# TensorE products with few contract rows are given 128 rows, the added ones zero

## The chip, the cores and the metric

The kernel runs on one core of a Trainium2 chip. The metric is the device time of one execution in microseconds (us). The times compared are those of executions without a profile; a profiled execution of this kernel is longer, and its page and trace serve to see what happens inside.

## What is computed

There are 16 graphs (B) of 1,024 nodes (N) with 64 features each (C). Cut to what matters, for each graph:

```python
h = maximum(layernorm(x), 0)
neigh = (adj > 0) & ~eye                      # neighbours of each node
rank = cumsum(neigh, -1) - neigh              # number of a neighbour along its row
nb = neigh.sum(-1)
skip = where(nb > 10, (nb + 1) // 2, 1)       # at least 1
rem = neigh & (skip > 1) & (rank % skip == skip - 1) & mask
rem = rem | transpose(rem)                    # edges dropped, in both directions
nd = (adj or eye) and not rem
s = sort(where(nd, h, inf))                   # per node and feature, over the neighbours left
agg = 0.25 * quantile(s, 0.25) + 0.5 * quantile(s, 0.5) + 0.25 * quantile(s, 0.75)
y = relu((h + agg) @ W1 + b1) @ W2 + b2       # 64 -> 128 -> 64
out = x + y * mask
```

The kernel does not sort dense rows. It turns each node's remaining neighbours into a short list of indices, gathers their features from a table in memory, and sorts those.

## The kernel before

The kernel is one program in which two streams are woven together: the preparation of the next graphs (load, number, drop, keep, order, collect) and the results of the graphs before (sorting networks on VectorE, then the dense layers). A scheduler fixes the order on each engine when the program is built. P is 128, NT is 8 (row tiles of a graph), HALF is 512, KEYS is 136 and PACKED is 332 columns.

The cuts below are the parts that the change and the prediction touch. A comment "L702" gives the line number under which the profile names the statement; these comments are added here.

Constants. `base` is zero outside its first two rows, and zero in those from column 136 on; `blocks` is 1 where the row's number is less than the column's; `ones16` is all ones, and in the program each has 128 rows.

```python
b2r = cst.tile([1, C], F32, name="b2r")
ones_r = cst.tile([1, P], F32, name="ones_r")
...
ident16, ones16, minus16, before16, base, blocks, own2 = (...)
```

Loading a graph: the sign of the adjacency, transposed by TensorE, with the diagonal taken off.

```python
nc.scalar.activation(sg, at, AF.Sign)                                   # L640
...
    nc.tensor.matmul(tp[:, s], sg[:, m * P:(m + 1) * P], ident16, ...)  # L646
if t // 4 == n:
    nc.tensor.matmul(tp[:, t % 4], minus16, ident16, ...)               # L651
...
nc.scalar.activation(to, tp, AF.Relu, saturate=False)                   # L656, to ne
```

Counting the neighbours of each node in each block of 128 columns (`cnt`, 8 rows) and in all (`nb`):

```python
counts[b] = wk.tile([NT, N], BF16, name="cnt", bufs=1)
...
for s in range(NT):
    nc.tensor.matmul(cp, one[:, 7 - s:15 - s], ne[:, s, cols], ...)     # L674
nc.scalar.copy(cnt[:, cols], cp)                                        # L675
...
for t in range(lo, hi):
    nc.tensor.matmul(nb[:, t:t + 1], cnt[:, t * P:(t + 1) * P], ones16[0:NT, 0:1], start=True, stop=True)  # L678
```

Dropping edges: a neighbour's number in its row is the count of the blocks before it (8 rows) and its number within the block.

```python
for n in range(2):
    rk = psum.tile([P, HALF], F32, name="rk", tag="mx", bufs=3)
    nc.tensor.matmul(
        rk, cnt[:, ts], blocks[0:NT, 4 * n:4 * n + 4, None].to_broadcast([NT, 4, P]), start=True, stop=False, ...
    )                                                                   # L702
    for s in range(4):
        nc.tensor.matmul(rk[:, s * P:(s + 1) * P], ne[:, 4 * n + s, ts], upper, ...)   # L707
    nc.scalar.activation(dist[:, n * HALF:(n + 1) * HALF], rk, AF.Abs, bias=...)       # L711
nc.vector.tensor_scalar(rem[:, t], dist, 1.0, half[:, t:t + 1], OP.add, OP.is_equal)   # L712
```

Collecting: the packed codes of each node's neighbours are put into the order of their numbers, on top of a base of keys (2 rows). VectorE takes the indices out of it.

```python
flat = psum.tile([P, PACKED], F32, name="codeP", tag="code", bufs=2)
nc.tensor.matmul(flat, ones16[0:2], base[0:2], start=True, stop=False)  # L790
for t in range(NT):
    nc.tensor.matmul(flat, perm[:, t, k * P:(k + 1) * P], pack[:, t], start=False, stop=(t == NT - 1))  # L792
nc.scalar.copy(st[:, k], flat[:, OWN:VALUES])                           # L795, then L799 and L800
...
nc.vector.max(keys[:, at:at + 8], left)                                 # L805
```

Gathers and sorting: `nc.gpsimd.indirect_dma_start` (L930) gathers one list place of 128 nodes; VectorE sorts (L961, L962), weighs (L969) and TensorE sums (L971).

The dense layers:

```python
for t in range(NT):
    nc.tensor.matmul(high, o[:, t, 0:2 * C], at[:, t], ...)             # L1051
for t in range(NT):
    nc.tensor.matmul(low, o[:, t, 2 * C:], at[:, t], ...)               # L1054, 64 columns
highs = wk.tile([P, HALF], F32, name="highs", bufs=1)
nc.scalar.copy(highs, high)
lows = wk.tile([C, HALF], F32, name="lows", bufs=1)
nc.scalar.copy(lows, low)
hp = psum.tile([P, HALF], F32, name="hp", tag="misc")
nc.tensor.matmul(hp, w1, highs, start=True, stop=False)                 # L1061
nc.tensor.matmul(hp, w1[0:C], lows, start=False, stop=True)             # L1062, 64 rows
...
nc.tensor.matmul(yp, ones_r, b2r[:, None, :].to_broadcast([1, n, C]), start=True, ...)  # L1074, 1 row
for k in range(n):
    nc.tensor.matmul(yp[:, k], h1[:, k * P:(k + 1) * P], w2, ...)       # L1078
```

A float32 matmul stands in the trace as two records, so the 32 products at L1061 are 64 there.

Of the kernel before, what the change touches and what calls it, by code (L numbers as in the profile page):

```python
# [27 lines left out]
F32 = mybir.dt.float32  # L28
F16 = mybir.dt.float16
BF16 = mybir.dt.bfloat16  # L30
# [9 lines left out]
P = 128  # L40
N = 1024
C = 64
H = 128
NT = N // P
# [490 lines left out]
def list_layer(  # L535
# [65 lines left out]
    w1 = cst.tile([P, H], F32, name="w1")  # L601
    w2 = cst.tile([H, C], F32, name="w2")
    b1c = cst.tile([H, 1], F32, name="b1c")
    b2r = cst.tile([1, C], F32, name="b2r")
    ones_r = cst.tile([1, P], F32, name="ones_r")

    def late_constants():

        nc.sync.dma_start(out=kf, in_=cf32[:, F32_AT:F32_AT + F32_PARTS[-1]])
        for n in range(2):  # L610
            nc.sync.dma_start(out=w1[n * C:(n + 1) * C], in_=W1)
        nc.sync.dma_start(out=w2, in_=W2)
        nc.sync.dma_start(out=b1c, in_=b1[:, None])
        nc.sync.dma_start(out=b2r, in_=b2[None, :])
        nc.vector.memset(ones_r, 1.0)

    over = cst.tile([P, 3, B, NT], F32, name="over")
# [5 lines left out]
    neT, nbs, rems, perms = {}, {}, {}, {}  # L623
    pack = cst.tile([P, NT, PACKED], BF16, name="pack")
    nc.vector.tensor_copy(pack[:, :, OWN:OWN + 2], own2.rearrange("p (t k) -> p t k", k=2))
    lists, owns, coefs, tables = {}, {}, {}, {}
    group_idx, group_own, group_num, group_tab, counts = {}, {}, {}, {}, {}

    def load(b, fast=False):

        ne = wk.tile([P, NT, N], FP8, name="ne", bufs=2)
        neT[b] = ne

        counts[b] = wk.tile([NT, N], BF16, name="cnt", bufs=1)
        nbs[b] = [wk.tile([P, NT], F32, name=n) for n in ("bias", "half")]
        for t in range(NT):
            ask(b, t)
            at = asked.pop((b, t))
            sg = wk.tile([P, N], BF16, name="sg")
            nc.scalar.activation(sg, at, AF.Sign)  # L640
            ask(*divmod(b * NT + t + 2, NT))
            for n in range(2):
                tp = psum.tile([P, 4, P], F32, name="tp", tag="mx", bufs=3)
                for s in range(4):
                    m = 4 * n + s
                    nc.tensor.matmul(  # L646
                        tp[:, s], sg[:, m * P:(m + 1) * P], ident16, start=(s == 0), stop=(s == 3 and t // 4 != n),
                        skip_group_check=True,
                    )
                if t // 4 == n:  # L650
                    nc.tensor.matmul(tp[:, t % 4], minus16, ident16, start=False, stop=True, skip_group_check=True)  # L651
                to = ne[:, 4 * n:4 * n + 4, t * P:(t + 1) * P]
                if fast:
                    nc.vector.tensor_scalar(to, tp, 0.0, None, OP.max, saturate=False)
                else:
                    nc.scalar.activation(to, tp, AF.Relu, saturate=False)  # L656
            if fast and t == 3:
                number(b, 0, 4)
            yield 0.1
        if fast:  # L660
            number(b, 4, NT)
        else:
            number(b, 0, NT)
        yield 1.4

    def number(b, lo, hi):

        ne, cnt = neT[b], counts[b]
        bias, half = (k[:, lo:hi] for k in nbs[b])
        for n in range(lo // 4, hi // 4):  # L670
            cols = slice(n * HALF, (n + 1) * HALF)
            cp = psum.tile([NT, HALF], F32, name="cp", tag="mx", bufs=3)
            for s in range(NT):
                nc.tensor.matmul(cp, one[:, 7 - s:15 - s], ne[:, s, cols], start=(s == 0), stop=(s == NT - 1))  # L674
            nc.scalar.copy(cnt[:, cols], cp)  # L675
        nb = psum.tile([P, NT], F32, name="nb", tag="misc")
        for t in range(lo, hi):
            nc.tensor.matmul(nb[:, t:t + 1], cnt[:, t * P:(t + 1) * P], ones16[0:NT, 0:1], start=True, stop=True)  # L678
        nb = nb[:, lo:hi]

        sk = wk.tile([P, NT], I32, name="sk")[:, lo:hi]
        nc.vector.tensor_scalar(sk, nb, 1.0, None, OP.add)
        many = wk.tile([P, NT], F32, name="many")[:, lo:hi]
        nc.vector.scalar_tensor_tensor(many, nb, 10.0, mask[:, b, lo:hi], OP.is_gt, OP.mult)
        nc.vector.tensor_scalar(sk, sk, 1, None, OP.logical_shift_right)
        nc.vector.tensor_scalar(bias, sk, -1.5, -2047.0, OP.mult, OP.add)
        nc.vector.tensor_scalar(half, sk, 0.5, 1.0, OP.mult, OP.add)
        nc.vector.tensor_tensor(half, half, many, OP.mult)

    def drop(b):  # L690

        ne = neT[b]
        bias, half = nbs[b]
        cnt = counts[b]
        rem = wk.tile([P, NT, N], BF16, name="rem", tag="wide", bufs=1)
        rems[b] = rem
        for t in range(NT):
            ts = slice(t * P, (t + 1) * P)
            dist = wk.tile([P, N], F16, name="dist")
            for n in range(2):  # L700
                rk = psum.tile([P, HALF], F32, name="rk", tag="mx", bufs=3)
                nc.tensor.matmul(  # L702
                    rk, cnt[:, ts], blocks[0:NT, 4 * n:4 * n + 4, None].to_broadcast([NT, 4, P]), start=True, stop=False,
                    skip_group_check=True,
                )
                for s in range(4):
                    nc.tensor.matmul(  # L707
                        rk[:, s * P:(s + 1) * P], ne[:, 4 * n + s, ts], upper, start=False, stop=(s == 3),
                        skip_group_check=True,
                    )  # L710
                nc.scalar.activation(dist[:, n * HALF:(n + 1) * HALF], rk, AF.Abs, bias=bias[:, t:t + 1])  # L711
            nc.vector.tensor_scalar(rem[:, t], dist, 1.0, half[:, t:t + 1], OP.add, OP.is_equal)  # L712
            yield 0.5
# [59 lines left out]
    def collect(b, parts=((0, NT),)):  # L773
# [12 lines left out]
        for first, last in parts:  # L786
            for k in range(first, last):
                flat = psum.tile([P, PACKED], F32, name="codeP", tag="code", bufs=2)
                code = flat[:, :KEYS].rearrange("p (s k) -> p s k", k=17)
                nc.tensor.matmul(flat, ones16[0:2], base[0:2], start=True, stop=False)  # L790
                for t in range(NT):
                    nc.tensor.matmul(  # L792
                        flat, perm[:, t, k * P:(k + 1) * P], pack[:, t], start=False, stop=(t == NT - 1)
                    )
                nc.scalar.copy(st[:, k], flat[:, OWN:VALUES])  # L795
                halves, bytes_ = (
                    own[:, k, b % 2].bitcast(d).rearrange("p (c k) -> p c k", c=C) for d in (BF16, U8)
                )
                nc.scalar.copy(halves[:, :, 1], flat[:, VALUES:VALUES + C])  # L799
                nc.scalar.copy(bytes_[:, :, 0:2], flat[:, VALUES + C:].rearrange("p (c k) -> p c k", k=2))  # L800
                left = code[:, :, :16]
                rest = wk.tile([P, NT, 16], F32, name="rest", bufs=1)
                lo, hi = PASSED[k], PASSED[k + 1]
                for at in range(lo, hi, 8):
                    nc.vector.max(keys[:, at:at + 8], left)  # L805
                    if at + 8 < hi:
                        nc.vector.match_replace(rest, keys[:, at:at + 8], left, 0.0)
                        left = rest
                yield 0.4 * (hi - lo) / 4 - 0.4
# [231 lines left out]
    def mlp(b, o):  # L1041
# [3 lines left out]
        for n in range(2):  # L1045
# [8 lines left out]
                nc.tensor.matmul(low, o[:, t, 2 * C:], at[:, t], start=(t == 0), stop=(t == NT - 1))  # L1054
            highs = wk.tile([P, HALF], F32, name="highs", bufs=1)
            nc.scalar.copy(highs, high)
            lows = wk.tile([C, HALF], F32, name="lows", bufs=1)
            nc.scalar.copy(lows, low)
            yield 1.0
            hp = psum.tile([P, HALF], F32, name="hp", tag="misc")  # L1060
            nc.tensor.matmul(hp, w1, highs, start=True, stop=False)  # L1061
            nc.tensor.matmul(hp, w1[0:C], lows, start=False, stop=True)  # L1062
            h1 = wk.tile([P, HALF], F32, name="h1", bufs=1)
            nc.scalar.activation(h1, hp, AF.Relu, bias=b1c)
            yield 1.0
# [5 lines left out]
    def output(h1, n, mask, x):  # L1071

        yp = psum.tile([P, n, C], F32, name="yp", tag="misc")
        nc.tensor.matmul(  # L1074
            yp, ones_r, b2r[:, None, :].to_broadcast([1, n, C]), start=True, stop=False, skip_group_check=True
        )
        for k in range(n):
            nc.tensor.matmul(  # L1078
                yp[:, k], h1[:, k * P:(k + 1) * P], w2, start=False, stop=(k == n - 1), skip_group_check=True
            )  # L1080
        nc.vector.tensor_tensor(yp, yp, mask[:, :, None].to_broadcast([P, n, C]), OP.mult)
        nc.vector.tensor_tensor(x, x, yp, OP.add)
# [323 lines left out]
```

## Time and profile before

| what | value |
|---|---|
| device time, median of 3 | 2027.63 us |
| lowest and highest | 2026.68 and 2040.0 us |
| span of the profiled execution | 2713.0 us |
| mean granted TensorE clock in it | 0.688 of full speed |

In the profile, PE is TensorE's matmuls and PEld its weight loads, DVE is VectorE, ACT is ScalarE, POOL is GpSimd and SP the engine that issues most transfers. A group's line reads: source line, engine, operation, output<-inputs, stationary rows*columns, rows x columns of the moving operand, type and count; then the busy time in us and the mean of one in ns; then the idle time of the engine ahead of it, and what ended most of it. In a timeline the first two numbers are the start and the duration in us; a bracket gives the idle time ahead on that engine. In records, the clock of TensorE is either full or half, and changes about every few to some hundred us. The chain is the work that ended last, followed back from the end through what released each step; "issue" in it is time in which an engine waited for nothing that the profile shows.

### The profile page before, as it was taken

What the parts mean: (1) busy time and instruction counts of PE and PEld (TensorE: products, weight loads), DVE (VectorE), ACT (ScalarE), POOL (GpSimd) and SP (SyncE); (2) the same over time, 40 slices, a digit from 0 to 9 for tenths busy, and PEclk for the clock granted to TensorE, in tenths of its full rate; (3) what the DMA queues carried; (4) which work ended last, traced back from release to release, by engine and by line L of the source; (5) the groups of instructions that cost most, each with busy time, mean ns of one, the idle gap of its engine ahead of it and who ended that gap; (6) DMA issues with size and microseconds to landing.
All of it is one profiled execution on the core that took longest, in us unless ns stands there. A gap on an engine that the chain in (4) does not pass through costs nothing.

```text
span 2713.0 us, 25381 instructions
## 1 busy us (share of the span) xinstructions
PE 1377.2 (51%) x8367; PEld 737.9 (27%) x8385; DVE 1162.5 (43%) x3634; ACT 926.9 (34%) x2414; POOL 1128.6 (42%) x1129
## 2 busy tenths in 40 slices
PE   7227163433664655645564555643565665514435
PEld 3114132211332323322232333322332323202223
DVE  2202255232322752453523652466633554338692
ACT  6247243323552533243342544232341532100101
POOL 0630726353325454455525355445325345537100
PEclk7657576665776767766687767756677677656767
DMA  3232212021222231212212121222111211111000
GB/s 99 64 79 72 59 47 61 14 71 45 78 53 47 48 84 24 67 49 66 48 37 59 43 73 37 55 65 49 53 42 24 62 23 19 30 22 22 20 0 11
DMA packets 152591, 130.12 MB, mean 48 GB/s; under 512 B 117570, under 2 KB 118082, under 8 KB 152450
## 3 DMA queue, kind: packets, MB, share of 16 engines
q1 hardware_dynamic: 116482, 91.51, 12.1%
q0 software_dynamic: 35968, 36.90, 8.0%
q8 instruction: 68, 1.11, 0.2%
q14 instruction: 73, 0.60, 0.1%
HBM read 112.78 MB, written 13.81 MB: 47 GB/s over the span
## 4 chain that ended last, share of the span: by engine, by line
PE 37%; another core or an unknown queue 33%; issue 11%; ACT 10%; DVE 8%; DMA 1%; POOL 0%; SPq 0%; POOLq 0%; DVEq 0%; ACTq 0%
PE codeP L792 6%; PE rk L707 3%; PE acc L971 3%; PE rk L702 3%; PE kp L727 2%; PE kp L724 2%; ACT dist L711 2%; PE kp L723 2%; PE tp L646 2%; ACT sg L640 2%; PE low L1054 2%; PE high L1051 2%; PE cp L674 2%; DVE g L962 2%
## 5 line engine op out<-in xcount | busy, mean ns | idle before, releaser
L930 POOL DMA_INDIRECT g<-htab,idx x1072 | 1072.7, 1001 | 1324.7 <-issue 376.7
L646 PE MATMUL tp<-kb,sg 128*128 128x128 bf16 x1024 | 123.4, 270 | 400.6 <-issue 138.4
L961 DVE TENSOR_TENSOR g<-g 128x768 f32<-128x768 f32 (+3 forms) x408 | 279.5, 702 | 88.1 <-DMA g<-htab,idx 81.2
L962 DVE TENSOR_TENSOR g<-g 128x512 f32<-128x512 f32 (+3 forms) x408 | 279.3, 701 | 20.2 <-PE tp L651 10.7
L711 ACT ACTIVATE dist<-rk,bias 128x512 f16<-128x512 f32 x256 | 172.4, 690 | 329.2 <-remote 188.9
L712 DVE TENSOR_SCALAR rem<-dist,half 128x1024 bf16<-128x1024 f16 x128 | 62.8, 491 | 421.6 <-ACT dist L711 387.2
L656 ACT ACTIVATE ne<-tp 128x512 fp8e4<-128x512 f32 x240 | 136.3, 600 | 310.8 <-remote 214.2
L971 PE MATMUL acc<-g,kf 128*128 128x256 f32 (+2 forms) x448 | 155.0, 495 | 162.1 <-DVE g L969 120.4
L702 PE MATMUL rk<-kb,cnt 8*128 8x512 bf16 x256 | 126.0, 492 | 176.6 <-ACT dist L711 100.8
L646 PEld LDWEIGHTS <-sg 128*128 128x128 bf16 x1024 | 93.0, 123 | 428.8 <-issue 244.1
L792 PE MATMUL codeP<-pack,perm 128*128 128x332 bf16 x1024 | 201.3, 342 | 9.5 <-DVE pause L941 6.3
L728 ACT ACTIVATE kept<-kp 128x512 fp8e4<-128x512 f32 x256 | 151.8, 600 | 122.7 <-remote 87.9
L731 PE MATMUL code<-kw,kept 128*128 128x17 fp8e5 x1024 | 67.3, 175 | 172.3 <-ACT kept L728 95.7
L971 PEld LDWEIGHTS acc<-g,kf 128*128 128x128 f32 x448 | 96.3, 256 | 191.5 <-DVE g L969 125.6
L707 PEld LDWEIGHTS <-ne 128*128 128x128 fp8e4 x1024 | 75.1, 114 | 262.2 <-issue 261.3
L640 ACT ACTIVATE sg<-at 128x1024 bf16<-128x1024 f32 x128 | 132.6, 1055 | 13.3 <-DMA at<-in_adj_dram 13.3
L792 PEld LDWEIGHTS <-perm 128*128 128x128 bf16 x1024 | 95.9, 106 | 150.0 <-issue 84.3
L707 PE MATMUL rk<-kw,ne 128*128 128x128 fp8e5 x1024 | 131.6, 265 | 0.0
L805 DVE MAX8 keys<-codeP 128x8 f32<-128x128 f32 x128 | 38.0, 297 | 205.2 <-ACT own L800 128.6
L1032 DVE TENSOR_SCALAR at_p<-iota,node 128x512 bf16<-128x512 f16 x256 | 77.4, 360 | 111.3 <-remote 86.9
L795 ACT CAST st<-codeP 128x4 bf16<-128x4 f32 x128 | 21.4, 167 | 294.6 <-PE codeP L792 139.9
L727 PE MATMUL kp<-kw,rem 128*128 128x128 fp8e5 x1024 | 118.0, 239 | 0.0
(155 smaller groups left out, 2315.2 us busy)
## 6 DMA issues: line engine op xcount, KB each, us to landing
at<-in_adj_dram SPq DMA_DIRECT2D x128, 512.0 KB
g<-htab,idx POOLq DMA_INDIRECT x1072
xt<-in_x_dram SPq DMA_DIRECT2D x16, 256.0 KB
htab<-xt SPq DMA_DIRECT2D x16, 256.0 KB
gtab<-xt SPq DMA_DIRECT2D x16, 256.0 KB
y<-in_x_dram SPq DMA_DIRECT2D x16, 256.0 KB
out_dram<-y SPq DMA_DIRECT2D x16, 256.0 KB
gg<-g SPq DMA_DIRECT2D x16, 96.0 KB
```

The source lines that it names most:

```text
L640: nc.scalar.activation(sg, at, AF.Sign)
L646: nc.tensor.matmul(tp[:, s], sg[:, m * P:(m + 1) * P], ident16, start=(s == 0), stop=(s == 3 and t // 4 != n), skip_group_check=True,)
L702: nc.tensor.matmul(rk, cnt[:, ts], blocks[0:NT, 4 * n:4 * n + 4, None].to_broadcast([NT, 4, P]), start=True, stop=False, skip_group_check= ...
L707: nc.tensor.matmul(rk[:, s * P:(s + 1) * P], ne[:, 4 * n + s, ts], upper, start=False, stop=(s == 3), skip_group_check=True,)
L711: nc.scalar.activation(dist[:, n * HALF:(n + 1) * HALF], rk, AF.Abs, bias=bias[:, t:t + 1])
L727: nc.tensor.matmul(kp[:, s], rem[:, t, at:at + P], minus, start=False, stop=(s == 3))
L728: nc.scalar.activation(kept[:, 4 * n:4 * n + 4], kp, AF.Relu, saturate=False)
L792: nc.tensor.matmul(flat, perm[:, t, k * P:(k + 1) * P], pack[:, t], start=False, stop=(t == NT - 1))
L930: nc.gpsimd.indirect_dma_start(out=g[:, slot, k - lo, h], out_offset=None, in_=tab, in_offset=bass.IndirectOffsetOnAxis(ap=idx[:, at:at + ...
L961: nc.vector.tensor_tensor(at(f, df, n), pa, pb, one)
L962: nc.vector.tensor_tensor(pa if back else pb, pa, pb, other)
L971: nc.tensor.matmul(acc, ident32, lines[:, s], start=False, stop=(s == now[-1] and not ends), skip_group_check=True)
```

## The change

Each product whose stationary operand had 1, 2 or 8 rows, and the one with 64, gets an operand of 128 rows; the rows added hold zeros in one of the two factors, so that the product is the same. For that, `cnt`, `lows` and `b2r` become constants that are cleared once and of which only the first rows are written. The base product of the keys no longer writes the 196 columns in which it is zero, 136 instead of 332. It is for TensorE to see products of one shape. The 64-row products of the small group at the end (L1134) are left as they are, as are those with few stationary columns (L674, L1054).

```diff
-    b2r = cst.tile([1, C], F32, name="b2r")
-    ones_r = cst.tile([1, P], F32, name="ones_r")
+    b2r = cst.tile([P, C], F32, name="b2r")
+    nc.vector.memset(b2r, 0.0)
+    ones_r = cst.tile([P, P], F32, name="ones_r")
+    lows = cst.tile([P, HALF], F32, name="lows")
+    nc.vector.memset(lows, 0.0)
...
-        nc.sync.dma_start(out=b2r, in_=b2[None, :])
+        nc.sync.dma_start(out=b2r[0:1], in_=b2[None, :])
...
+    cnt = cst.tile([P, N], BF16, name="cnt")
+    nc.vector.memset(cnt, 0.0)
...
-        counts[b] = wk.tile([NT, N], BF16, name="cnt", bufs=1)
...
-            nc.scalar.copy(cnt[:, cols], cp)
+            nc.scalar.copy(cnt[0:NT, cols], cp)
...
-            nc.tensor.matmul(nb[:, t:t + 1], cnt[:, t * P:(t + 1) * P], ones16[0:NT, 0:1], start=True, stop=True)
+            nc.tensor.matmul(nb[:, t:t + 1], cnt[:, t * P:(t + 1) * P], ones16[:, 0:1], start=True, stop=True)
...
-                    rk, cnt[:, ts], blocks[0:NT, 4 * n:4 * n + 4, None].to_broadcast([NT, 4, P]), start=True, stop=False,
+                    rk, cnt[:, ts], blocks[:, 4 * n:4 * n + 4, None].to_broadcast([P, 4, P]), start=True, stop=False,
...
-                nc.tensor.matmul(flat, ones16[0:2], base[0:2], start=True, stop=False)
+                nc.tensor.matmul(
+                    flat[:, :KEYS], ones16, base[:, :KEYS], start=True, stop=False, skip_group_check=True
+                )
                 for t in range(NT):
                     nc.tensor.matmul(
-                        flat, perm[:, t, k * P:(k + 1) * P], pack[:, t], start=False, stop=(t == NT - 1)
+                        flat, perm[:, t, k * P:(k + 1) * P], pack[:, t], start=False, stop=(t == NT - 1),
+                        skip_group_check=True,
                     )
...
-            lows = wk.tile([C, HALF], F32, name="lows", bufs=1)
-            nc.scalar.copy(lows, low)
+            nc.scalar.copy(lows[0:C], low)
...
-            nc.tensor.matmul(hp, w1[0:C], lows, start=False, stop=True)
+            nc.tensor.matmul(hp, w1, lows, start=False, stop=True)
...
-            yp, ones_r, b2r[:, None, :].to_broadcast([1, n, C]), start=True, stop=False, skip_group_check=True
+            yp, ones_r, b2r[:, None, :].to_broadcast([P, n, C]), start=True, stop=False, skip_group_check=True
```

More of the change, by code (lines that the diff above doesn't have):

```diff
@@ L625, in list_layer @@
     nc.vector.tensor_copy(pack[:, :, OWN:OWN + 2], own2.rearrange("p (t k) -> p t k", k=2))
+    cnt = cst.tile([P, N], BF16, name="cnt")
+    nc.vector.memset(cnt, 0.0)
     lists, owns, coefs, tables = {}, {}, {}, {}
-    group_idx, group_own, group_num, group_tab, counts = {}, {}, {}, {}, {}
+    group_idx, group_own, group_num, group_tab = {}, {}, {}, {}
     def load(b, fast=False):
@@ L666, in number @@
     def number(b, lo, hi):
-        ne, cnt = neT[b], counts[b]
+        ne = neT[b]
         bias, half = (k[:, lo:hi] for k in nbs[b])
@@ L693, in drop @@
         bias, half = nbs[b]
-        cnt = counts[b]
         rem = wk.tile([P, NT, N], BF16, name="rem", tag="wide", bufs=1)
```

## The prediction

> **What bounds the kernel now.** I first read the page's table of engines: no engine is busy for more than half of the profiled span, so no sum of busy time can be the time.
>
> ```profile
> span 2713.0 us, 25381 instructions
> PE 1377.2 (51%) x8367; PEld 737.9 (27%) x8385; DVE 1162.5 (43%) x3634; ACT 926.9 (34%) x2414; POOL 1128.6 (42%) x1129
> ```
>
> One warning goes with it: the profiled execution took 2713 us, the timed ones 2027.63. Some 686 us of the profile are the recording's own. I therefore take from the profile durations and intervals of single instructions, which repeat to a few ns, and not shares of the span.
>
> Second I read the chain that ended last, to see which engine's work is on the path.
>
> ```profile
> PE 37%; another core or an unknown queue 33%; issue 11%; ACT 10%; DVE 8%; DMA 1%; POOL 0%; SPq 0%; POOLq 0%; DVEq 0%; ACTq 0%
> PE codeP L792 6%; PE rk L707 3%; PE acc L971 3%; PE rk L702 3%; PE kp L727 2%; PE kp L724 2%; ACT dist L711 2%; PE kp L723 2%; PE tp L646 2%; ACT sg L640 2%; PE low L1054 2%; PE high L1051 2%; PE cp L674 2%; DVE g L962 2%
> ```
>
> Among the engines TensorE carries the chain: 37% of 2713 us are 1004 us, nearly three quarters of its 1377 us of busy time. The two dearest places are the ones that the change edits: codeP (L790, L792) and rk (L702, L707). The 44% under an unknown queue or "issue" are time in which the profile names no worker; where the missing 686 us lie I can't tell, but this is the likely place.
>
> Third I read the groups by form, for the narrow products and their neighbours.
>
> ```profile
> L792 PE MATMUL codeP<-pack,perm 128*128 128x332 bf16 x1024 | 201.3, 342 | 9.5 <-DVE pause L941 6.3 <-DVE perm L769 2.6 <-issue 0.4
> L707 PE MATMUL rk<-kw,ne 128*128 128x128 fp8e5 x1024 | 131.6, 265 | 0.0
> L702 PE MATMUL rk<-kb,cnt 8*128 8x512 bf16 x256 | 126.0, 492 | 176.6 <-ACT dist L711 100.8 <-issue 51.1 <-ACT ne L656 24.4
> L790 PE MATMUL codeP<-kb 2*128 2x332 bf16 x128 | 42.2, 330 | 116.8 <-DVE keys L805 40.6 <-issue 39.1 <-DVE rest L807 35.2
> ```
>
> The form "8*128" is 8 stationary rows by 128 columns. A mean of one matmul is the latency of a pipelined instruction, so I price by intervals between starts, from the timeline. First a stretch at half clock, matmuls and then weight loads:
>
> ```profile
> 1005.08 0.61 PE L707 MATMUL rk<-kw,ne 128*128 128x128 fp8e5 x4
> 1005.48 1.06 PE L646 MATMUL tp<-kb,sg 128*128 128x128 bf16 x8
> 1006.33 0.31 PE L651 MATMUL tp<-kb 128*128 128x128 bf16 x1
> 1006.58 0.60 PE L702 MATMUL rk<-kb,cnt 8*128 8x512 bf16 x1
> 1007.11 0.61 PE L707 MATMUL rk<-kw,ne 128*128 128x128 fp8e5 x4
> 1007.65 0.60 PE L702 MATMUL rk<-kb,cnt 8*128 8x512 bf16 x1
> ...
> 1006.23 0.15 PEld L651 LDWEIGHTS <-kb 128*128 128x128 bf16 x1
> 1006.57 0.10 PEld L702 LDWEIGHTS <-cnt 8*128 8x128 bf16 x1 [0.20 <-issue]
> 1007.11 0.34 PEld L707 LDWEIGHTS <-ne 128*128 128x128 fp8e4 x4 [0.44 <-issue]
> ```
>
> Eight 128-row matmuls of 128 columns take 1006.33 - 1005.48 = 0.85 us, 0.106 each; the load of L651 begins 0.10 us ahead of its matmul, so it lies beside the previous one. The single L651 ahead of L702 takes 1006.58 - 1006.33 = 0.25 us: 0.14 too much. The load of L702 begins only with its own matmul (1006.57, after 0.20 us without a load). L702 itself, 512 columns, takes 0.53 us where four times 0.106 are 0.43: 0.10 too much, and again the next load (L707) waits until 1007.11. One narrow matmul costs about 0.24 us more than a full one of the same columns.
>
> Then a stretch at full clock:
>
> ```profile
> 700.97 1.31 PE L792 MATMUL codeP<-pack,perm 128*128 128x332 bf16 x8
> 702.22 0.31 PE L790 MATMUL codeP<-kb 2*128 2x332 bf16 x1
> 702.46 1.31 PE L792 MATMUL codeP<-pack,perm 128*128 128x332 bf16 x8
> 703.70 0.31 PE L790 MATMUL codeP<-kb 2*128 2x332 bf16 x1
> ```
>
> L790 to L792 takes 0.24 us. The median between two adjacent L792 of the same columns, counted over 690 pairs at full clock, is 143 ns; so 0.10 is excess after the narrow matmul, and 702.22 - 700.97 = 1.25 against 8 x 0.143 = 1.14 shows 0.10 before it.
>
> **What the Trainium skill says.** "TensorEngine Tiling (Array Packing)", section "Key Properties": changing the tiling mode, not just the tile, drains TensorE. It gives no duration; that a matmul of few rows changes the mode by itself is my reading, and the excess on both sides in the trace agrees with it. "TensorE: Matmul & The Clock Gate", section "LDWEIGHTS (loading the stationary operand)": a load goes by its columns, and 32 rows load no faster than 128. The trace agrees: 94 ns on average for L702's 8 rows, 106 for L792's 128. The same page, "What happens when you issue a matmul", says that the next weights are loaded during the running matmul, which is what the loads between full matmuls do and those at a narrow one don't. Its "Back-to-back issue gap" has a matmul paid by its moving columns; so more rows of zeros should cost nothing.
>
> **The change, part by part.** Excess per narrow matmul, as medians of intervals in the whole trace (in, out):
> - L702, 8 rows, x256. Half clock: in 246 - 107 = 139 ns, out 535 - 427 = 108; together 247. Full clock: in 152 - 56 = 96, out 317 - 216 = 101; together 197. Of the 232 that L707 follows at once, 132 ran at half clock (57%): mean 225 ns, x256 = 58 us.
> - L790, 2 rows, x128. Full clock: 94 + 99 = 193; half: 140 + 111 = 251; 78% at full clock: 206 ns, 26 us. Its columns fall from 332 to 136: 196 columns at 143/332 = 0.43 ns are 84 ns at full, 275/332 = 0.83 make 162 at half clock; mean 101 ns, 13 us. The t = 0 matmul over all 332 columns is unchanged.
> - L1074, 1 row, 34 pairs: in 309 - 216 = 93, out 304 - 216 = 88; 6 us. L1062, 64 rows, 32 pairs: from L1061 523 ns, where L1061 to itself has 533: no gain inside; out 522 - 427 = 95; 3 us. Float32 loads there are exposed anyway.
> - L678, 8 rows, 16 groups: L674 has 8 columns, L678 needs 128, so a change of form stays between them (312 against 216 ns). One change out is saved at most: 2 us. L1054 with its 64 columns (309 against 216 after L1051) stays as it is.
> - Added: three clears, about a microsecond of VectorE at the start while inputs arrive.
>
> Sum: 58 + 26 + 13 + 6 + 3 + 2 = 108 us of TensorE time. What lies on the path? Of L702 and L707 the chain holds 78 + 84 of 126 + 132 us, 63%; of L790 and L792 27 + 153 of 42 + 201, 74%; about 70% for the rest. So 58 x 0.63 = 36, 39 x 0.74 = 29, 11 x 0.7 = 8: 73 us.
>
> From this I take a fifth, because of the first rival, and predict 58 us: 2027.6 - 58 = 1970 us.
>
> **What moves.** The instructions are the same in number but for the clears; their order is not. Set side by side, about 2,500 of VectorE's 6,475 and 1,700 of ScalarE's 2,843 stand elsewhere, and in TensorE's queue the runs of L1051 go from 70 to 81, of L1054 from 50 to 72, of L971 from 83 to 71. The scheduler gives narrow matmuls another price, and the weaving of two batches comes out differently. Queues run in order, so a worse weave costs waits anywhere. For this I allow 20 to 30 us either way.
>
> **Rivals.**
> First, ScalarE takes over in the drop stage. For one tile there it does two dist (690 ns), two ne (600) and one sg (1055): 3.6 us. TensorE needs 2 x (0.53 + 0.54) + 0.96 = 3.1 us at half clock. If it holds throughout, the 58 us of rk are hidden and some 37 us remain on the path: about 1990. For it: rk waits 100.8 us for dist. Against it: from 1001 to 1009 TensorE is busy for 7.10 of 8 us and ScalarE for 5.61, and ne or sg isn't there for every tile.
> Second, GpSimd's gathers are the bound: 1,072 of them at 1,001 ns. Then at most the last stages gain: about 2010. For it: it works while the others stand still (858 to 869). Against: it also waits long for VectorE's idx (300.7 us), and the chain holds no POOL.
> Third, zeros aren't free or the new weave is bad: 2030 to 2060. Nothing in the profile shows a row's price; I hold the weave possible and small.
> Fourth, the waits that a late TensorE causes in two woven streams multiply: all 108 us and more come back, 1900 to 1920. TensorE's share of the chain supports it mildly.
>
> **Range and chances.** 1970 in the middle; the weave and the first rival give a spread of about 35 us: 1920 to 2016 should hold it 8 times in 10. The mark for 2% is 1987, half a spread away: faster 0.69, within 2% 0.25, slower 0.06.
>
> **What would show it.** In the changed profile the load of L702's successor should begin ahead of its matmul, with no 0.20 and 0.44 us before loads; L702 to L707 should be 216 or 427 ns, L790 to L792 about 60 or 115 ns, and TensorE's busy time should fall by roughly 100 us. Wrong would be the mechanism if those intervals stay; wrong would be the path if they shrink and the time doesn't, and then ScalarE's or GpSimd's row should be unchanged in the waits; the weave is to blame if waits appear at lines without any narrow matmul.

## Result: 2030.68 to 1976.03 us, and the profile after

| kernel | device time, median | ratio to before, 95% interval |
|---|---|---|
| before | 2030.68 us | |
| after | 1976.03 us | 0.9725, 0.9678 to 0.9772 |

The gain is 55 us, or 2.75%.

Two views of the kernel after show what became of the narrow products. First the timeline at half clock, in a stretch like the one that the prediction read (matmuls, then weight loads; start and duration in us, then the instruction; L702 and L707 are now L706 and L711, L646 and L651 are L651 and L656):

```profile
145.62 0.31 PE L656 MATMUL tp<-kb 128*128 128x128 bf16 x1
145.73 0.63 PE L706 MATMUL rk<-kb,cnt 128*128 128x512 bf16 x1
146.15 0.63 PE L711 MATMUL rk<-kw,ne 128*128 128x128 fp8e5 x4
146.58 0.63 PE L706 MATMUL rk<-kb,cnt 128*128 128x512 bf16 x1
...
145.62 0.15 PEld L706 LDWEIGHTS <-cnt 128*128 128x128 bf16 x1
145.73 0.15 PEld L711 LDWEIGHTS <-ne 128*128 128x128 fp8e4 x1
146.15 0.36 PEld L711 LDWEIGHTS <-ne 128*128 128x128 fp8e4 x3 [0.28 <-issue]
```

The load of L706 begins at 145.62, together with the matmul before its own; the first load of L711 begins with L706. From L656 to L706 it is 0.11 us (before: 0.25), from L706 to L711 0.42 (before: 0.53). One group of rk goes from 1.07 to 0.85 us. What matters is which load lies beside which matmul, not whether a bracket stands there: the 0.28 us ahead of the last three loads lies beside L706 itself, and no matmul is late for it. It is so in the whole traces: the load of L702 begins within 20 ns of its own matmul in 168 of 174 pairs that follow a 128-row matmul closely (counted in before_again, below), while that of L706 is never less than 53 ns ahead, in 157 pairs.

Then the timeline at full clock in the collect stage (L790 and L792 are now L794 and L798):

```profile
770.78 1.30 PE L798 MATMUL codeP<-pack,perm 128*128 128x332 bf16 x8
771.92 0.22 PE L794 MATMUL codeP<-kb 128*128 128x136 bf16 x1
771.98 1.30 PE L798 MATMUL codeP<-pack,perm 128*128 128x332 bf16 x8
```

A base product and its eight followers take 1.20 us (771.98 - 770.78) where they took 1.49.

The whole-trace medians say the same. L706 to L711 is 215 ns at full clock and 426 at half (were 317 and 535), L794 to L798 59 at full clock (was 242; 160 in the run below in which only its columns fall, so about 100 of the 183 belong to the rows). L711 to L706 is 107 ns at half clock (was 247). At full clock it is 56 where the two follow at once (was 152); many pairs stand at 106 or about 197 there, though the weights are loaded as early in them, so that what they wait for is something else.

Now the page of after: engines, and the chain.

```profile
span 1979.1 us, 25408 instructions
PE 1147.2 (58%) x8369; PEld 705.8 (36%) x8385; DVE 1167.4 (59%) x3637; ACT 912.2 (46%) x2414; POOL 1165.0 (59%) x1129
POOL 0372753777377776777767776762777377771000
PE 7%; POOL 5%; DVE 5%; issue 4%; DMA 1%; ACT 0%; POOLq 0%; DVEq 0%
```

This span is that of the timed runs, while the profile of before shown ahead of the prediction was 686 us longer than its own, so the two can't be subtracted. The row of POOL's busy tenths differs as well. In that profile it was

```profile
POOL 0630726353325454455525355445325345537100
```

and now it is 7 in most slices, which is all that a closed line of gathers can show, 1.03 us busy in each 1.33. The chain adds up to 22% only and ends early; it is of no use for shares here.

### The profile page after: what moved, and what is told of

It is laid out like the page before. It is cut to its first block, busy times and chain, and to the rows that moved or that the text cites. A ratio compares the mean times of both kernels' runs of the same rounds, so it can differ in the third digit from the quotient of the medians.

```text
span 1979.1 us, 25408 instructions
## 1 busy us (share of the span) xinstructions
PE 1147.2 (58%) x8369; PEld 705.8 (36%) x8385; DVE 1167.4 (59%) x3637; ACT 912.2 (46%) x2414; POOL 1165.0 (59%) x1129
## 5 line engine op out<-in xcount | busy, mean ns | idle before, releaser
L937 POOL DMA_INDIRECT g<-htab,idx x1072 | 1108.3, 1034 | 610.0 <-issue 313.0
L798 PE MATMUL codeP<-pack,perm 128*128 128x332 bf16 x1024 | 175.9, 312 | 33.4 <-DVE pause L948 32.0
L651 PE MATMUL tp<-kb,sg 128*128 128x128 bf16 x1024 | 109.5, 247 | 107.5 <-ACT sg L645 90.6
L728 PE MATMUL kp<-rem,kw 128*128 128x512 bf16 x256 | 99.2, 388 | 99.9 <-DVE rem L716 53.2
L798 PEld LDWEIGHTS <-perm 128*128 128x128 bf16 x1024 | 91.8, 99 | 135.9 <-issue 48.8
L731 PEld LDWEIGHTS <-rem 128*128 128x128 bf16 x1024 | 81.3, 98 | 147.4 <-issue 105.3
L706 PE MATMUL rk<-kb,cnt 128*128 128x512 bf16 x256 | 110.1, 430 | 38.0 <-ACT dist L715 24.4
L651 PEld LDWEIGHTS <-sg 128*128 128x128 bf16 x1024 | 82.7, 112 | 131.2 <-ACT sg L645 100.5
L711 PEld LDWEIGHTS <-ne 128*128 128x128 fp8e4 x1024 | 88.5, 108 | 89.2 <-issue 65.1
L1058 PE MATMUL high<-at_p,o 128*128 128x512 bf16 x240 | 69.6, 401 | 81.6 <-DVE at_p L1039 80.5
L711 PE MATMUL rk<-kw,ne 128*128 128x128 fp8e5 x1024 | 115.0, 239 | 0.0
L990 ACT CAST o<-acc 128x512 bf16<-128x512 f32 x48 | 28.3, 589 | 179.2 <-PE acc L978 171.1
```

The costliest lines, as they stand in the source:

```text
L731: nc.tensor.matmul(kp[:, s], rem[:, t, at:at + P], minus, start=False, stop=(s == 3))
L937: nc.gpsimd.indirect_dma_start(out=g[:, slot, k - lo, h], out_offset=None, in_=tab, in_offset=bass.IndirectOffsetOnAxis(ap=idx[:, at:at + ...
```

## Experiments

Twelve runs, of nine kernels, were made in four sets; in two of these the unchanged kernel took 2031 and 2032 us and in the other two 2673 and 2675 us, so a ratio is compared only with ratios of the same kind of set, and each table below is of one kind.

### The kernel before once more

No edit.

> The kernel before once more, unchanged, for a second profile of it. If the 686 us by which the first profiled span was longer than the timed runs were the recording's own, this span is near 2030 us, the share of an unknown queue in the chain falls from 33% to under 5%, and GpSimd's gathers then stand as closely as after the change, 1.33 us from start to start. The rival, that the gaps belong to the kernel's order, has them again at the same places. Time ratio 1.00 in both.

Measured: 1.0005 (0.9984 to 1.0026), a span of 2026.5 us. Page of this run (engines, POOL's tenths, chain):

```profile
span 2026.5 us, 25381 instructions
PE 1286.0 (63%) x8367; PEld 709.0 (35%) x8385; DVE 1166.2 (58%) x3634; ACT 913.8 (45%) x2414; POOL 1159.4 (57%) x1129
POOL 0371762777165777577747776771757777770000
PE 13%; POOL 8%; issue 5%; DVE 4%; ACT 1%; DMA 1%; POOLq 0%; DVEq 0%
```

The unknown queue is gone from the chain, and GpSimd's gathers stand closely. This is the profile that after is to be compared with. TensorE's busy time falls from 1286.0 to 1147.2, by 139 us; the others hardly move (DVE +1, ACT -2, POOL +6). But the span falls by 47. The groups that issue gathers (L930, L1143) and the VectorE group that sorts what they bring (L961) show what became of it (busy us, mean ns, then the idle time of the engine ahead of them and what ended it). Before:

```profile
L930 POOL DMA_INDIRECT g<-htab,idx x1072 | 1105.6, 1031 | 654.2 <-issue 316.4 <-DVE idx L834 166.4 <-DVE at_p L1032 75.2
L1143 POOL DMA_INDIRECT out_dram<-gx,gto x4 | 4.8, 1204 | 191.4 <-DMA out_dram<-y 185.8 <-PE kp L727 2.8 <-DMA out_dram<-gx,gto 2.5
L961 DVE TENSOR_TENSOR g<-g 128x768 f32<-128x768 f32 (+3 forms) x408 | 280.2, 702 | 374.7 <-DMA g<-htab,idx 367.3
```

After:

```profile
L937 POOL DMA_INDIRECT g<-htab,idx x1072 | 1108.3, 1034 | 610.0 <-issue 313.0 <-DVE idx L841 166.2 <-PE tp L651 67.8
L1149 POOL DMA_INDIRECT out_dram<-gx,gto x4 | 4.1, 1026 | 182.6 <-DMA out_dram<-y 179.3 <-DMA out_dram<-gx,gto 3.0 <-issue 0.3
L968 DVE TENSOR_TENSOR g<-g 128x768 f32<-128x768 f32 (+3 forms) x408 | 280.4, 703 | 430.3 <-DMA g<-htab,idx 423.9
```

The 1,072 gathers cost 1106 and 1108 us, plus some 315 us at 0.30 us of "issue" between two: 1.33 us from start to start, unchanged. GpSimd's idle time in these two groups falls from 845.6 to 792.6 us, by 53, and the span by 47. What got shorter are the waits ahead of a new batch of gathers, for lists and for free buffers (with the engines named by inference, so I read their sum only), and the wait at the end for the last outputs (186 to 179 us). The first gather begins at 74.6 us instead of 80.8. So the time is a line of gathers with fixed pitch, its waits for the rest, and a tail. This sum alone doesn't make GpSimd the bound: it would come out for every engine whose work is unchanged, VectorE too. What speaks for the gathers is the third line: with TensorE shorter, VectorE's longest wait, the one for gathered rows, grows from 367 to 424 us (411 in rows_only, below, where no instruction is moved). If they are the bound, what TensorE saves counts only where GpSimd is waiting or has finished; taking gathers off it, below, tests that.

### The parts by themselves, where before takes 2031 us

Rows only: all products on 128 rows, the base product over 332 columns. The order of instructions on TensorE, GpSimd and VectorE is exactly that of before, but for the three clears; on ScalarE the 32 copies at L1058 stand in the same places on another line.

```diff
 # after, changed back in one place
-                nc.tensor.matmul(flat[:, :KEYS], ones16, base[:, :KEYS], start=True, stop=False, ...)
+                nc.tensor.matmul(flat, ones16, base, start=True, stop=False, ...)
```

> Every narrow product gets 128 rows, the base product keeps its 332 columns. The order on every engine is that of before (but for the three clears). Theory, narrow products cost two array changes each: TensorE is shorter by 58 + 26 + 6 + 3 + 2 = 95 us, some two thirds of it on the path: ratio 0.965 to 0.980. Rival, the gain is the new order's: ratio 0.995 to 1.005.

Columns only: before, with the base product over 136 columns. The order on TensorE and GpSimd is exactly that of after.

```diff
-                nc.tensor.matmul(flat, ones16[0:2], base[0:2], start=True, stop=False)
+                nc.tensor.matmul(flat[:, :KEYS], ones16[0:2], base[0:2, :KEYS], start=True, stop=False, ...)
```

> Only the base product's columns fall from 332 to 136; all narrow products stay narrow. The order on every engine is that of after. Theory, narrow products cost: TensorE is shorter by 13 us at most, and the order may add 20 us either way: ratio 0.985 to 1.005. Rival, the gain is the new order's: ratio 0.970 to 0.980, as the whole change.

Rows only again, in a later set:

> All narrow products on 128 rows in the order of before, base product over 332 columns. Where before takes about 2030 us: 0.976 to 0.984 as at first. Where before takes about 2670 us: the relieved kernels differ by 59 us for the same edit; if the gathers hide part of the saving, fewer than 59 us here (ratio over 0.980); if they don't, 55 to 65 us (0.976 to 0.980).

| kernel | order | ratio | TensorE busy | mean clock |
|---|---|---|---|---|
| before_again | before | 1.0005 (0.9984 to 1.0026) | 1286.0 us | 0.761 |
| rows_only | before | 0.9802 (0.9764 to 0.9840) | 1161.2 | 0.781 |
| rows_only_2 | before | 0.9810 (0.9773 to 0.9848) | 1158.7 | 0.785 |
| cols_only | after | 0.9920 (0.9894 to 0.9945) | 1269.4 | 0.762 |
| after | after | 0.9725 (0.9678 to 0.9772) | 1147.2 | 0.788 |

Rows bring 39 to 40 us with no instruction moved; that is the main part, just short of the range expected (0.965 to 0.980), and the rival that the gain is the new order's falls. Columns, with all of the new order, bring 16 us, as much as TensorE's busy time falls there (16.6). 0.9802 x 0.9920 = 0.9724: the two add up to the whole. The second rows_only repeats the first; rows alone were not measured where before takes 2673 us.

The cols_only run also corrects what the prediction said of the order. Rows alone move nothing. It is the base product's columns, 332 or 136, that make the scheduler weave the streams anew.

### Full width for the columns as well

The kernel after, and the products with 8 and 64 stationary columns get 128. For `low` they are columns 64 to 191 of the three terms: its first 64 output rows are not used, the last 64 are the term wanted. `one_w` is `one` widened with zero columns, and the tiles `cp` and `low` get 128 rows.

```diff
-                nc.tensor.matmul(cp, one[:, 7 - s:15 - s], ne[:, s, cols], ...)
+                nc.tensor.matmul(cp, one_w[:, 7 - s:7 - s + P], ne[:, s, cols], ...)
-                nc.tensor.matmul(low, o[:, t, 2 * C:], at[:, t], ...)
+                nc.tensor.matmul(low, o[:, t, C:], at[:, t], ...)
-            nc.scalar.copy(lows[0:C], low)
+            nc.scalar.copy(lows[C:], low[C:])
```

> The kernel after, and the products with 8 and 64 stationary columns (L674, L1054 of before) get 128 columns too, in the same order as after. Theory, every change of the array's form costs about 0.1 us in and 0.1 us out: about 32 groups of each kind, some 12 us less of TensorE; 309 ns between high and low become 216; ratio to before 0.963 to 0.972, that is 4 to 12 us under after. Rival, changes of columns are not of that kind, or GpSimd's gathers hide it: within 3 us of after.

Measured: 0.9722 (0.9682 to 0.9762), 1975.67 us: the same as after. The cost is there all the same. Timeline of this run, the two products by turns:

```profile
995.61 0.38 PE L1065 MATMUL low<-at_p,o 128*128 128x512 bf16 x1
995.82 0.38 PE L1062 MATMUL high<-at_p,o 128*128 128x512 bf16 x1
996.04 0.38 PE L1065 MATMUL low<-at_p,o 128*128 128x512 bf16 x1
```

And of before_again, where the product has 64 columns:

```profile
1058.27 0.40 PE L1054 MATMUL low<-at_p,o 128*64 128x512 bf16 x1
1058.61 0.39 PE L1051 MATMUL high<-at_p,o 128*128 128x512 bf16 x1
1058.93 0.40 PE L1054 MATMUL low<-at_p,o 128*64 128x512 bf16 x1
```

Each step by turns takes 0.33 us with 64 columns and 0.22 with 128 (medians from high to low: 309 and 216 ns). So few columns cost about 0.1 us at each change, as few rows do. But TensorE's busy time falls by 8 us at most (1147.2 to 1139.2; twelve records of `low` are missing in the second trace), and none of it can be told in the time. The expectation, 4 to 12 us, is not borne out; that the gathers hide it is the rival's reading, and fits, but the interval of 0.4% either way would not show a gain of a few us.

### Taking gathers off GpSimd

224 of the 1,072 gathers (each fourth list place) become plain loads of 128 fixed rows of the same table by SyncE. This leaves out the lookup by index for them; the bytes are the same.

```diff
                         at = PASSED[k] + s
+                        if s % 4 == 3:
+                            nc.sync.dma_start(out=g[:, slot, k - lo, h], in_=tab[FRONT + k * P:FRONT + k * P + P])
+                            continue
                         nc.gpsimd.indirect_dma_start(...)
```

With the rows widened, where before takes 2032 us:

> All narrow products on 128 rows, 224 of the 1,072 gathers replaced by plain loads of fixed rows (the lookup by index is left out for them). Where before takes about 2030 us: if GpSimd's gathers are the backbone, 224 x 1.33 = 298 us of them fall away and 100 to 250 us come off the 1991 us of rows_only, ratio 0.86 to 0.93; if TensorE is, at most 40 us, ratio over 0.96. Where before takes about 2670 us: 0.904 to 0.913 as in the run before.

Measured: 0.8813 (0.8769 to 0.8857), 1792.9 us. That is 200 us under rows_only_2 of the same set (1993.04). Page of this run:

```profile
span 1793.9 us, 25533 instructions
PE 1146.9 (64%) x8364; PEld 702.2 (39%) x8385; DVE 1159.5 (65%) x3637; ACT 916.8 (51%) x2414; POOL 953.7 (53%) x905
```

TensorE, VectorE and ScalarE have as much to do as in rows_only (1161.2, 1164.7, 907.1) and the time still falls by 200 of the 298 us (224 x 1.33) taken off GpSimd. To compare: 125 us off TensorE brought 40. A microsecond of GpSimd is worth two thirds of one, a microsecond of TensorE one third. The order of the streams is another here too, so this is a size and not a clean slope. It shows that the gathers weigh more than TensorE's work, and VectorE's wait for gathered rows falls with them, from 411 us in rows_only to 182. Whether more of TensorE's saving comes through beside fewer gathers would need before with the same relief in this kind of set, which was not run.

The same edit on before and on rows_only, in one set of the 2673 kind:

> The kernel before, but 224 of the 1,072 gathers on GpSimd (every fourth list place) are replaced by plain loads of 128 fixed rows of the same table, issued by SyncE: the lookup by index is left out for them, the bytes are the same. Theory, GpSimd's chain of gathers (1.33 us from start to start) is the backbone and hides most of TensorE's time: 224 x 1.33 = 298 us of GpSimd fall away, the time falls by 100 to 250 us (1780 to 1930). Rival, TensorE is the backbone: the time stays within 40 us of before.

> The same relief of GpSimd, with all narrow products given 128 rows, in the same order on every engine as the relieved kernel before. Theory, gathers hide TensorE's saving: with GpSimd relieved more of it comes through than the 36 us of rows_only, 50 to 100 us against the relieved kernel before. Rival, what isn't seen in rows_only is hidden by VectorE, ScalarE or waits between the two streams: again 30 to 45 us.

| kernel, where before takes 2673 us | median | ratio |
|---|---|---|
| relief_before | 2488.41 us | 0.9329 (0.9285 to 0.9374) |
| relief_rows | 2428.99 us | 0.9082 (0.9036 to 0.9128) |

Relief brings 185 us here, and rows bring 59 us on top, in the same order on every engine; both lie in the ranges expected. The expectation asked whether more comes through than the 40 us of rows_only; but the 40 were measured in the 2031 kind, and no rows_only ran in this one. Whether the relief or the long kind lets more through stays open.

### Single products back to few rows, where before takes 2673 us

Each is the kernel after with one product narrow again, in exactly after's order.

```diff
 # rk_narrow
-                    rk, cnt[:, ts], blocks[:, 4 * n:4 * n + 4, None].to_broadcast([P, 4, P]), ...
+                    rk, cnt[0:NT, ts], blocks[0:NT, 4 * n:4 * n + 4, None].to_broadcast([NT, 4, P]), ...
 # base_narrow
-                    flat[:, :KEYS], ones16, base[:, :KEYS], ...
+                    flat[:, :KEYS], ones16[0:2], base[0:2, :KEYS], ...
```

> The kernel after, but the 256 products of block counts at rk have 8 rows again; the same order on every engine as after. Prediction's terms: 58 us of TensorE, 36 on the path: 25 to 45 us above after, ratio to before 0.985 to 0.995. Rival, ScalarE bounds the drop stage and hides it: under 15 us above after, ratio below 0.980.

> The kernel after, but the 128 base products of keys have 2 rows again, over 136 columns; the same order on every engine as after. Prediction's terms: 26 us of TensorE, 19 on the path: 10 to 25 us above after, ratio to before 0.977 to 0.985. Rival, VectorE's keys bound the collect stage: under 5 us above after.

These two stood without after beside them, so after was run under the same conditions, with rk_narrow again:

> The kernel after, unchanged, beside a new run of rk_narrow, so that both stand under the same conditions. Where before takes about 2030 us: ratio to before 0.968 to 0.977 as at first. Where before takes about 2670 us, with the semaphores held up while GpSimd writes gathers, less is hidden behind the gathers: ratio 0.955 to 0.975, 70 to 120 us.

> The kernel after with the 256 products at rk on 8 rows again, in after's order. Where before takes about 2030 us: 25 to 45 us above after if the prediction's term holds, under 15 us if ScalarE or GpSimd hides it. Where before takes about 2670 us: ratio to before 0.998 to 1.002 as in the run before, 40 to 70 us above after.

| kernel | median | ratio | TensorE busy |
|---|---|---|---|
| rk_narrow (first set) | 2670.81 us | 0.9996 (0.9975 to 1.0016) | 1314.0 us |
| base_narrow (first set) | 2658.73 | 0.9929 (0.9901 to 0.9957) | 1264.9 |
| after_again (second set) | 2626.90 | 0.9821 (0.9779 to 0.9863) | 1234.5 |
| rk_narrow_2 (second set) | 2668.33 | 0.9980 (0.9957 to 1.0004) | 1317.0 |

Against the ratios expected, three of the four miss. rk_narrow and base_narrow lie above their ranges (0.985 to 0.995 and 0.977 to 0.985), and after_again gains 48 us where 70 to 120 were expected: the thought that in this kind less would be hidden behind the gathers is not borne out.

The rows of rk are worth 41 us (2668.33 - 2626.90), those of the base product about 0.0108 x 2675 = 29 us, with some 0.5% of uncertainty each. TensorE's busy time differs by about 80 us for rk (1314.0 and 1317.0 against 1234.5) where the prediction's term says 58, and by 30 for the base product, where it says 26. The 41 and 29 us are together more than the 48 us of the whole change here, so the rest of it (dense layers, columns, order) would have to cost some 20 us, or the uncertainty covers it; this isn't settled. ScalarE as the bound of the drop stage, which would have made rk_narrow equal to after, falls in this kind. For the 2031 kind the split between rk and base was not measured.

## Why the prediction was right, and where it wasn't

The predicted 1970 us stand against 1976 measured, 58 us of gain against 55. The mechanism is as predicted, but that the size fits so well is luck: two errors cancel, TensorE's saving being too small (108 us for 139) and the share of it that comes through too large (54% for 40%).

**The price of a narrow product holds.** 96 and 101 ns at full clock and 139 and 108 at half vanish, to within a few ns, wherever the two products follow at once, and after's intervals are the ones named beforehand (216 or 427, about 60). That more rows of zeros cost nothing shows in the same intervals: 512 columns take 215 ns with 128 rows. As the Trainium skill's "TensorE: Matmul & The Clock Gate", section "Back-to-back issue gap", has it, columns pay: its formula for a single gap gives about 216 ns. Its other figure, 131 ns for a sustained stream of 512 columns, isn't what this trace shows. That the cost is a drain at a change of tiling mode, the prediction's reading, no run shows; what they show is the late load and its price. One term doesn't hold: for L1074 I had a way in of 309 - 216 = 93 ns, but it fell to 293 only.

**TensorE's 108 us were too few.** Busy time fell by 139 us. Of this, rows took 125 where the terms say 95. Part of the surplus is the clock. In rows_only the instructions and their order are the same, yet about 7,100 of 8,367 matmuls began at full clock instead of 6,600, and unedited groups got shorter: cp (L674 before) from 74.8 to 67.7 us. Why the clock was full more often was not tested. Another part is L1062, where I saw no gain inside: L1061 to L1062 was 522 ns and is 429, L1062 to itself was 533 and is 429. With the way out, that is three intervals of about 0.1 us in 32 pairs, 9 us where the sum had 3. The 533 of L1061 to itself, by which I had judged it, was itself no clean measure: it mostly stands behind `low` with its 64 columns, and in full_width, where `low` has 128, it is 430.

**The share on the path was wrong.** 63 to 74% of TensorE's time, less a fifth, came from the chain of a profile that doesn't describe the timed runs. What came through is 55 of 139 us, 40%. The step that failed is the share on the path, and with it the reason for the discount, ScalarE in the drop stage. It is true in small part: in rows_only rk waits 100.8 us for dist where before_again has 81.5, but in after it is 24.4. The gathers on GpSimd account better for the rest: 298 us less of them brought 200 (relief_rows_2), while 125 us less of TensorE brought 40 and made VectorE wait 44 us longer for gathered rows (367 to 411). That was the second rival. I put it aside because the chain held no POOL and because GpSimd waited 300.7 us for idx. In the undisturbed profile that wait is 166.4 us and the chain holds 8% of POOL. The rival's size (2010) was wrong too: the gathers leave more of the gain than that. GpSimd itself waits for lists that TensorE helps to make, which would explain it and was not tested by itself.

**"The recording's own" was wrong.** The recorded execution of before_again spans 2026.5 us and that of after 1979.1, as long as timed ones, so the remark at the start that a profiled execution of this kernel is longer doesn't hold either. The 2713 us are close to what before takes in the long sets (2649 to 2696 us), and show the same late hand-overs (last section).

**"The scheduler gives narrow matmuls another price" was wrong**: rows moved nothing, columns did. The 20 to 30 us allowed for a new weave were not used up: columns and new order together came to 16 us of gain, where columns alone were priced at 13 us of TensorE.

## What to carry to other kernels

Where single products with few contract rows or few stationary columns stand between full ones, pad them to 128: in this kernel each product of few rows cost 0.2 us (0.25 at half clock) for nothing, as its weights and those of the next were not loaded beside the matmul before. For columns the intervals shrank likewise, but no gain in time was measured. How much of it reaches the time depends on what else bounds the kernel; here it was about a third for rows. Look at the start of the weight load against the start of the matmul before; a mean duration doesn't show it. And before a saving is weighed by the chain of a profile, compare that profile's span with the timed runs: a span a third too long is another execution, and its path isn't the one that is being timed.

## What the runs showed that I had not expected

The same kernel ran at two speeds, 2031 and 2673 us, by the set of runs. The instructions of TensorE, VectorE and ScalarE last the same in both (dist 690 ns, rk's intervals equal). What differs is the hand-over between engines. From the long profile of before, ScalarE's timeline and TensorE's around one of the gaps:

```profile
853.88 0.74 PE L1008 MATMUL acc<-g,kf 128*128 128x128 f32 x2
871.01 0.59 PE L646 MATMUL tp<-kb,sg 128*128 128x128 bf16 x4 [16.39 <-ACT dist L711]
...
852.74 0.60 ACT L656 ACTIVATE ne<-tp 128x512 fp8e4<-128x512 f32 x1 [5.75 <-remote]
870.27 0.69 ACT L711 ACTIVATE dist<-rk,bias 128x512 f16<-128x512 f32 x1 [15.98 <-remote]
```

The last matmul ahead of the gap ends at 854.62 us (853.88 + 0.74), and a dist, whose wait is for TensorE's semaphore, starts at 870.27; "remote" means that no instruction's end fits the semaphore's change. In between GpSimd issues a gather each 1.25 us. I measured, for each ScalarE instruction that raises a semaphore, the time from its end to the next change of that semaphore. In the long profile this is 4.2 us on average where GpSimd is writing a gather or has ended one within 0.7 us, and 0.02 us elsewhere; in before_again it is 0.01 us in both. VectorE (1.8 and 0.01 us) and TensorE (3.3 and 0.04 us) show it as well, and so does after_again, the other kernel in a long set (ScalarE 4.0 and 0.02 us). So in the long kind, semaphores change late while gathers are being written; that GpSimd's work and the others' thereby exclude each other to a large part is how I read it. What makes an execution of this kind is not known. Each of the four sets was wholly of one kind; both long sets ran on the same chip and the two short ones on two others, so that the chip is one candidate, untested. The change is worth 1.8% there (0.9779 to 0.9863) and 2.75% in the other kind.
